# One queue position for the products of v, a larger allowance for table lookups, and earlier weight sums and row turns in a fused attention and feed-forward kernel

## The chip, the cores and the metric

The kernel runs on one core of a Trainium2 chip, as one launch. The metric is the device time of that launch in microseconds: the median of three runs of the kernel before is 1821.81 us (1821.67 to 1823.17). Besides these runs there is one execution with the hardware profiler, from which all lines below come.

The core has a matrix engine (TensorE, PE in the profile, with PEld for its weight loads), a vector engine (VectorE, DVE), an activation engine (ScalarE, ACT), a general engine (GpSimd, POOL) and a queue that issues most transfers (SyncE, SP). Each works through its own instructions in the written order and waits on semaphores of the others.

## The reference

All data are f32. `x` is 16 x 256 x 512, `ctx` the same shape, the mask 16 x 1 x 512 of ones (the kernel still applies it).

```python
x = x + xattn(layernorm(x), ctx, mask, mask, Wq, bq, Wk, bk, Wv, bv)   # 16 heads of 16 channels
x = x + ffn(layernorm(x), lut, gate_idx, up_idx, down_idx)

# xattn: q, k, v = W @ input + b;  dot = q.k / 4 per head, masked
#        out = softmax(dot, over s) * mask @ v
# ffn:   w = lut[idx]  (a table of 16 values; 1376 x 512 indices each for gate and up, 512 x 1376 for down)
#        h = silu(x @ gate.T) * (x @ up.T);  out = h @ down.T
```

So the kernel has to look up 2.1 million weights in a table of 16 values, run 256 attention heads of 512 x 512 scores, and run a feed-forward layer with an inner width of 1376 over 4096 rows.

## The kernel before, in words

**Attention.** A unit (`u`, 64 of them) is four heads of one of the 16 batches; it has four steps, one for each 128 rows (256 steps, `s` from 0 to 255). In each step `scores(sa, sb)` (L469) issues two things side by side on TensorE, which holds four 32-row tiles: the scores `pa` of step `sa = s + 7` (L487), from which VectorE takes row maxima `nm` (L503, two reductions a step), and the turned scores `pb` of step `sb = s` (L495), which ScalarE exponentiates into `pt` (L507, four a step). The maximum enters `pb` as an extra row of `qp`. `turn_max(u)` (L509 to L515) turns a unit's maxima with a small product `pmx` (L512), VectorE copies it out as `mx` (L514), and a transfer issued by GpSimd (L515) writes it into `qp`, three steps before it is needed.

Between the scores of two steps stands a lump of other TensorE work: `apply_v` (L529, twice a unit), projections of q and k (L413, pq and pk), and in step `4u - 3` the pair `turn_max(u)` and `project_v` (L413, pv). The lists `lumps[s]` and `after[s]` are filled by hand and run in the order in which they were filled. `project_v` ends in a ScalarE copy `vt` (L453) and a GpSimd addition (L454). All these products take turns in four PSUM banks (`ps_b`); `pa` has two buffers of its own (`ps_a`). Every eighth step GpSimd multiplies and adds finished rows (`finish_rows`, L584 and L585).

**Lookups.** `look_up` makes weights from indices with VectorE alone: four bit masks (L146, L150), eight leaves (L157) and seven joins (L161, COPY_PREDICATED). Up to step `turns - 3` = 229 the pieces are wide, 128 x 688 (`lookups_early`); what is left of them at step 229 is issued there at once, `load_rest` then issues the load of the first piece of 128 x 344 (`idx_r`, L705), and `lookups_late` goes on. How many lookup operations a step gets is decided by `credit` (L767): each step adds 1930 ns plus `lasting[s]` (the lumps) and takes off `taken[s]` (other VectorE work) and 2590 ns for the reductions.

**Feed-forward.** The rows are eight blocks of 512 rows. Gate and up are done for pairs of blocks `p` = 0 to 3 and column groups `o` of 128 (the last has 96): the column group 0 of the first four blocks by plain products (`gate_up`, L914), everything else by `unit(p, o)`, which has seven products of half the depth in place of eight (L934), in the order 1, 6, 2, 7, 5, 4, 3, with VectorE additions (L938) between them. This needs sums of weights (`combine_w`, L830: `sw` and a changed `wu`) and sums of turned rows for each pair (`combine_x`, L839 to L842: `xe` and a changed `xT`). Product 6 needs the second of the four sums of both, product 7 the third sum of weights.

`fill(ns)` hands out VectorE work from the generator `between()`: sums of weights by column ranges (128 to 384, 384 to 688, then 688 to 1024 after five lookups, 1024 to 1376 after five more, and 0 to 128 last), and lookups between and after them. It adds `ns` to `room[0]`, which is cut to 3000, and issues work until the room is used up. Where a column group needs sums that are not issued yet, a loop in front of the unit (`while o not in ready`) issues all that is missing at once; that can happen for `o` 5 and 8. The units run in the order (0,1), (1,1), (0,2), ... (1,7), then pair 0 with `o` 8 to 10, pair 1 with 8 to 10, then pairs 2 and 3 with all of theirs; the fourteenth counted from zero is (0,8), the nineteenth is (1,10), the twentieth (2,0). Each unit runs three hooks: after product 6, after product 7 and after product 4. `turn_blocks` puts the norm and turning of the rows of a later pair into such hooks: nine steps, the last of which turns the last rows and then issues the four operations of `combine_x`.

After that comes the down product (L1121, L1140, L1145), which the change leaves as it is.

Of the kernel before, what the change touches and what calls it, by code (L numbers as in the profile page):

```python
# [19 lines left out]
def kernel(  # L20
# [46 lines left out]
    NU = 2 * NK  # L67
# [117 lines left out]
    def load_x2(k):  # L185
        x2s[k] = rpool.tile([P, T], F32, tag="x2", name=f"x2t_{k}", bufs=4)
        nc.sync.dma_start(x2s[k], x2_d[k])
        return x2s[k]
# [30 lines left out]
    with ExitStack() as att:  # L219
# [53 lines left out]
        def load_b(b):  # L273
            xn = p2.tile([P, NCC, T], F32, tag="xn", name=f"xn_{b}")
            nc.sync.dma_start(xn, x[b].rearrange("(o p) t -> p o t", p=P))
            cx = p2.tile([P, NCC, T], F32, tag="ctx", name=f"ctx_{b}")
            nc.sync.dma_start(cx, src[b].rearrange("(o p) t -> p o t", p=P))
            mb = p2.tile([P, T], F32, tag="mb", name=f"mb_{b}")
            nc.sync.dma_start(mb, mask[b, 0].partition_broadcast(P))
            inp[b] = (cx, xn, mb)  # L280

        def norm1(b, eng):
            xn = inp[b][1]
            for o in range(NCC):
                i = b * NCC + o
                eng.tensor_scalar(
                    xn[:, o, :], xn[:, o, :], rstd1[:, i : i + 1], nmr1[:, i : i + 1],
                    ALU.mult, ALU.add,
                )
# [30 lines left out]
        for i, w in enumerate((bq, bk)):  # L320
            for e in range(2):
                at = 64 * i + 32 * e
# [6 lines left out]
        for i, w in enumerate((bq, bk)):  # L329
            at = n + NCC * i  # L330
# [114 lines left out]
        def project_v(k, i):  # L445

            b, half = divmod(k, 2)
            cx = inp[b][0]
            c = 2 * half + i
            ps = ps_b.tile([P, 512], F32, tag="b", name=f"pv_{b}_{c}")  # L450
            in_columns(ps[:, :C], lambda o, at: cx[:, o, at], c * P, lambda o: wv[:, o, :])
            vt = p2.tile([P, C], F32, tag="vt", name=f"vt_{b}_{c}")
            nc.scalar.copy(vt, ps[:, :C])  # L453
            nc.gpsimd.tensor_tensor(  # L454
                vas[b % 2][:, c, :, 0:D], vt.rearrange("p (h d) -> p h d", d=D),
                bvb.rearrange("p (h d) -> p h d", d=D), ALU.add,
            )

        def mask_v(k, i):
            b, half = divmod(k, 2)  # L460
            c = 2 * half + i
            va = vas[b % 2][:, c, :, 0:D]
            m = cols[:, b * NCH + c : b * NCH + c + 1]
            nc.scalar.activation(va, va, AF.Copy, scale=m)
# [44 lines left out]
        def turn_max(u):  # L509
            ps = ps_b.tile([P, 512], F32, tag="b", name=f"pmx_{u}")  # L510
            nms.pop(u)
            nc.tensor.matmul(ps[:32, :P], nm32[u % 2], ident, start=True, stop=True)  # L512
            mx = p2.tile([4 * NCH, P], F32, tag="mx", name=f"mx_{u}")
            nc.vector.tensor_copy(mx, ps[: 4 * NCH, :P])  # L514
            nc.gpsimd.dma_start(qps[u % 4][17 : P : 32, :].rearrange("j (c t) -> j c t", t=P), mx)  # L515
# [73 lines left out]
        lumps, after = defaultdict(list), defaultdict(list)  # L589
# [32 lines left out]
            after[t + 18].append(lambda k=k: spread_sums(k))  # L622
            after[t + 20].append(lambda k=k: finish_rows(k))

        for u in range(NU):
            lumps[4 * u - 3].append(lambda u=u: turn_max(u))
        lumps[-3].append(lambda: project_v(0, 0))
        lumps[-2] += [lambda: project_v(0, 1), lambda: project_v(1, 0)]
        lumps[-1].append(lambda: project_v(1, 1))
# [1 line left out]
        for k in range(2, NK):  # L631
            for i in range(2):
                lumps[8 * k - 15 + 4 * i].append(lambda k=k, i=i: project_v(k, i))
                after[8 * k - 13 + 4 * i].append(lambda k=k, i=i: mask_v(k, i))
        for b in range(2, B):
            after[16 * b - 31].append(lambda b=b: load_b(b))
            after[16 * b - 23].append(lambda b=b: norm1(b, nc.gpsimd))
# [8 lines left out]
        taken = defaultdict(float)  # L646
# [55 lines left out]
        def load_rest():  # L702
            w, idx, h, k = rest[0]
            its[0] = lp.tile([P, WIDE], I32, tag="idx", name=f"idx_r{len(rest)}", bufs=2)
            nc.sync.dma_start(its[0][:, :PIECE], idx[h * P : (h + 1) * P, k * PIECE : (k + 1) * PIECE])  # L705
# [19 lines left out]
        credit = 0.0  # L725
# [16 lines left out]
        lasting = defaultdict(float)  # L742
# [9 lines left out]
        for s in range(min(min(after), min(lumps)), NSTEP + 2):  # L752
            sa = s + AHEAD if 0 <= s + AHEAD < NSTEP else None
            sb = s if 0 <= s < NSTEP else None
            if sa is not None or sb is not None:
                scores(sa, sb)
            for fn in lumps.pop(s, ()):
                fn()
            for fn in after.pop(s, ()):
                fn()  # L760
            if s >= 0:
                if s == turns - 3:
                    for _, op in early:
                        op()
                    load_rest()
                queue = early if s < turns - 3 else late
                credit += 1930 + lasting[s] - taken[s] - (2590 if sa is not None else -500)  # L767
                credit = min(credit, 1500.0)
                if s == NSTEP - 6:
                    closing.append(s)  # L770
                while credit > 0:
                    ns, op = next(queue, (0, None))
                    if op is None:
                        break
                    op()
                    credit -= ns
# [18 lines left out]
    with ExitStack() as ffn:  # L795
# [14 lines left out]
        def rows_of(o):  # L810
            return min(P, INTER - o * P)
# [22 lines left out]
        def combine_x(p):  # L834

            x1, x2 = xTs[2 * p], xTs[2 * p + 1]
            b11, b21, b12, b22 = x1[:, 0:2], x1[:, 2:4], x2[:, 0:2], x2[:, 2:4]
            xe = xes[p] = xep.tile([P, 3, 2, 4 * P], F32, tag="xe", name=f"xe_{p}")
            yield v.tensor_tensor(xe[:, 0], b22, b12, ALU.subtract)  # L839
            yield v.tensor_tensor(b12, b12, b11, ALU.subtract)  # L840
            yield v.tensor_tensor(xe[:, 1], b22, b12, ALU.subtract)
            yield v.tensor_tensor(xe[:, 2], b21, xe[:, 1], ALU.subtract)  # L842
# [53 lines left out]
        def fill(ns):  # L896

            room[0] = min(room[0] + ns, 3000.0)
            while room[0] > 0:
                took, op = next(todo, (0, None))  # L900
                if op is None:
                    break
                op()
                room[0] -= took


        def gate_up(n, o):

            rows = rows_of(o)
            at = slice(o * P, o * P + rows)  # L910
            ps = ps_a.tile([P, 2, 512], F32, tag="a", name=f"pgu_{n}_{o}")
            for i, w in enumerate((wg, wu)):
                for h in range(NH):
                    nc.tensor.matmul(  # L914
                        ps[:rows, i, :], w[:, h, at], xTs[n][:, h, :],
                        start=(h == 0), stop=(h == NH - 1),
                    )
            sg = rpool.tile([P, 4 * P], F32, tag="us0", name=f"sg_{n}_{o}", bufs=5)
            nc.scalar.activation(sg[:rows], ps[:rows, 0, :], AF.Silu)
            ht = f1.tile([P, 4 * P], F32, tag="ht", name=f"ht_{n}_{o}")  # L920
            v.tensor_tensor(ht[:rows], sg[:rows], ps[:rows, 1, :], ALU.mult)
            store_h(n, o, ht, rows)
# [49 lines left out]
        order = [(p, o) for o in range(1, 8) for p in range(2)]  # L972
        order += [(p, o) for p in range(2) for o in range(8, NO)]
        order += [(p, o) for p in range(2, 4) for o in range(NO)]
        hooks = defaultdict(list)

        def turn_blocks(n, at):

            k = 4 * n

            def step(i):
                if i:
                    turn2(k + i - 1)
                if i < 8:
                    norm2(k + i)
                    room[0] -= 550
                if i + 3 < 8:
                    load_x2(k + i + 3)
                if i == 8:
                    for _ in combine_x(n // 2):  # L990
                        room[0] -= 1230

            for i in range(3):
                hooks[at - 1, 2].append(lambda i=i: load_x2(k + i))
            for i in range(9):
                hooks[at + i // 3, i % 3].append(lambda i=i: step(i))

        turn_blocks(4, order.index((1, 8)))
        turn_blocks(6, order.index((2, 5)))
        for i in range(8):  # L1000
            for n, at in ((4, 8), (6, 15)):
                hooks[at + i, 0].append(lambda k=4 * n + i: load_x2(k))
# [5 lines left out]
        k = 4 * FIRST  # L1008
# [3 lines left out]
            fn()  # L1012
        load_x2(k + 2)
        load_x2(k + 3)
        gate_up(0, 0)
        gate_up(1, 0)
        turn2(k)
# [7 lines left out]
        gate_up(2, 0)  # L1025
        turn2(k + 2)
        turn2(k + 3)
        fill(6000)
        gate_up(3, 0)
        for _ in combine_x(1):  # L1030
            pass
        fill(3000)

        def run(fns):
            for fn in fns:
# [201 lines left out]
```

## Time and profile before

| what | value |
|---|---|
| median of three runs | 1821.81 us |
| the profiled execution, its own time | 1821.44 us |
| its span, first to last instruction | 1819.7 us |
| TensorE busy | 1796.0 us (99%) |
| VectorE busy | 1459.0 us (80%) |
| ScalarE / GpSimd busy | 799.5 / 491.5 us |
| attention, first feed-forward product | to about 993 us |
| units of gate and up | about 1025 to 1540 us |
| granted TensorE clock | 0.999 over the span |

The span is 1.7 us shorter than the execution's own time, and 2.1 us shorter than the median. The parts of the page that matter here are the busy times, the chain of work that ended last, and the waits; the timeline shows single instructions. A line of the timeline has the start in us, the duration in us, the engine, the line of the kernel, the operation, what it writes and reads, how many follow each other, and in brackets the idle time of the engine before it and what ended it. TensorE instructions overlap, so a group's duration is the stretch that it covers.

### The profile page before, as it was taken

The page shows a single profiled execution, that of the slowest core. Times are in us where ns is not written, and L with a number is a line of the kernel's source. Part 1 is how long each engine was busy: PE and PEld are TensorE (multiplying, and loading weights), DVE is VectorE, ACT ScalarE, POOL GpSimd, SP SyncE. Part 2 cuts the span into 40 slices and gives each one's busy share as a digit, 9 for nine tenths or more (in the row PEclk, how much of TensorE's full clock was granted, in tenths as well). Part 3 has the DMA queues.
Part 4 walks back from the last instruction along what each step waited for, and adds up shares of the span by engine and source line. Part 5 has one row for each costly group of instructions (what it writes and reads, how often), then busy time and mean ns, then how long its engine had stood idle before and what let it go on. Part 6 is the DMA issues. An engine that isn't in the chain of part 4 may idle for free.

```text
span 1819.7 us, 28550 instructions
## 1 busy us (share of the span) xinstructions
PE 1796.0 (99%) x10914; PEld 812.4 (45%) x10914; DVE 1459.0 (80%) x2030; ACT 799.5 (44%) x1523; POOL 491.5 (27%) x467
## 2 busy tenths in 40 slices
PE   8999999999999999999999999999999999999999
PEld 4333333333333333333234444444444444588887
DVE  6898988889898889898886799998888995353352
ACT  1777777777777777777676111112121111000000
POOL 4333343434333433433322122222222222000000
PEclk9999999999999999999999999999999999999999
DMA  6445534333433344444242211223231311533541
GB/s 187 129 143 149 149 115 129 121 114 96 127 114 125 92 128 137 148 121 141 87 120 75 69 58 55 74 81 106 68 104 42 116 51 44 182 132 126 176 132 58
DMA packets 118825, 201.07 MB, mean 111 GB/s; under 512 B 21781, under 2 KB 23961, under 8 KB 118689
## 3 DMA queue, kind: packets, MB, share of 16 engines
q1 hardware_dynamic: 114416, 196.21, 34.1%
q0 software_dynamic: 3168, 1.86, 0.5%
q8 instruction: 86, 1.41, 0.3%
q10 hardware_dynamic: 1104, 1.19, 0.2%
q14 instruction: 51, 0.41, 0.1%
HBM read 135.83 MB, written 58.10 MB: 107 GB/s over the span
## 4 chain that ended last, share of the span: by engine, by line
PE 92%; DVE 4%; DMA 1%; issue 0%; ACT 0%; SPq 0%; POOL 0%; ACTq 0%; DVEq 0%; POOLq 0%
PE p L934 27%; PE pa L487 15%; PE pv L529 12%; PE pb L495 11%; PE q L1140 11%; PE pv L413 3%; PE pq L413 3%; PE pk L413 3%; PE po L1121 2%; DVE nm L503 2%; PE q L1145 1%; PE pgu L914 1%; PE pmx L512 1%; PE pt L215 1%; DMA x2t<-x 1%; DVE chosen L161 0%
## 5 line engine op out<-in xcount | busy, mean ns | idle before, releaser
L503 DVE TENSOR_REDUCE nm<-pa 128x2 f32<-128x1024 f32 x512 | 603.3, 1220 | 103.8 <-PE pb L495 97.5
L507 ACT ACTIVATE pt<-pb 128x512 f32<-128x512 f32 x1024 | 530.0, 603 | 108.8 <-PE pb L495 107.7
L487 PE MATMUL pa<-kp,qp 32*128 32x512 f32 x2048 | 515.0, 616 | 9.5 <-DVE nm L503 6.9
L495 PE MATMUL pb<-qp,kp 32*128 32x512 f32 x2048 | 514.9, 617 | 0.0
L487 PEld LDWEIGHTS pa<-kp,qp 32*128 32x128 f32 x2048 | 179.5, 184 | 208.7 <-DVE nm L503 163.1
L529 PE MATMUL pv<-pt,va 128*32 128x512 f32 x2048 | 246.2, 598 | 0.0
L495 PEld LDWEIGHTS pb<-qp,kp 32*128 32x128 f32 x2048 | 203.4, 183 | 83.5 <-issue 52.4
L934 PE MATMUL p<-xe,wu 128*128 128x512 f32 (+1 forms) x336 | 158.1, 593 | 1.0 <-DVE w L938 1.0
L934 PE MATMUL p<-xT,sw 128*128 128x512 f32 (+1 forms) x336 | 157.9, 592 | 0.0
L934 PE MATMUL p<-xT,wg 128*128 128x512 f32 (+1 forms) x336 | 157.9, 592 | 0.0
L961 POOL TENSOR_TENSOR ha<-ha,sg 128x512 f32<-128x512 f32 (+1 forms) x42 | 60.4, 1438 | 344.3 <-DVE ha L938 326.0
L966 ACT ACTIVATE w<-w 128x512 f32<-128x512 f32 (+1 forms) x42 | 26.5, 630 | 241.4 <-DVE w L938 241.4
L529 PEld LDWEIGHTS pv<-pt,va 128*32 128x32 f32 x2048 | 53.4, 109 | 173.1 <-ACT pt L507 97.1
L515 POOL DMA_DIRECT2D qp<-mx x64 | 37.8, 591 | 313.1 <-DVE mx L514 290.4
L1156 ACT COPY q<-q 128x256 f32<-128x256 f32 x14 | 5.2, 372 | 254.4 <-PE q L1140 254.4
L534 ACT COPY us<-pv 128x512 f32<-128x512 f32 x128 | 74.9, 585 | 91.7 <-PE pv L529 91.0
L934 PEld LDWEIGHTS p<-xe,wu 128*128 128x128 f32 (+1 forms) x336 | 62.8, 187 | 83.0 <-issue 71.3
L934 PEld LDWEIGHTS p<-xT,wg 128*128 128x128 f32 (+1 forms) x336 | 62.7, 187 | 79.2 <-issue 75.4
L934 PEld LDWEIGHTS p<-xT,sw 128*128 128x128 f32 (+1 forms) x336 | 62.1, 187 | 75.4 <-issue 73.9
L948 ACT ACTIVATE sg<-sg 128x512 f32<-128x512 f32 (+1 forms) x42 | 26.5, 631 | 152.4 <-DVE sg L938 152.4
L541 POOL TENSOR_TENSOR us<-us,us 128x512 f32<-128x512 f32 x64 | 82.3, 1286 | 16.5 <-ACT us L534 16.5
L429 POOL TENSOR_TENSOR natk<-natk,mb 128x512 f32<-128x512 f32 x31 | 40.0, 1289 | 157.7 <-ACT natk L426 152.0
(205 smaller groups left out, 2375.1 us busy)
## 6 DMA issues: line engine op xcount, KB each, us to landing
x2t<-x SPq DMA_DIRECT2D x96, 256.0 KB
h<-h SPq DMA_DIRECT2D x7, 2560.0 KB
kp<-kd SPq DMA_DIRECT2D x62, 256.0 KB
qp<-qd SPq DMA_DIRECT2D x62, 256.0 KB
h<-ha SPq DMA_DIRECT2D x38, 256.0 KB
h<-hb SPq DMA_DIRECT2D x38, 256.0 KB
rb<-rd SPq DMA_DIRECT2D x32, 256.0 KB
xr<-in_x_dram SPq DMA_DIRECT2D x32, 256.0 KB
```

The source lines that it names most:

```text
L413: nc.tensor.matmul(ps[32 * j : 32 * j + 32], weights(o, slice(first + 32 * j, first + 32 * j + 32)), moving(o), start=(o == 0), stop=(o == ...
L429: nc.gpsimd.tensor_tensor(t, t, mb, ALU.mult)
L487: nc.tensor.matmul(pa[:, jj, :], qps[ua % 4][at, ca * P : (ca + 1) * P], kps[ua % 4][at, :], start=True, stop=True,)
L495: nc.tensor.matmul(pb, kps[ub % 4][at, cb * P : (cb + 1) * P], qps[ub % 4][at, :], start=True, stop=True,)
L503: nc.vector.tensor_reduce(nms[ua][:, 2 * half : 2 * half + 2, ca], pa, AX.X, ALU.max, negate=True)
L507: nc.scalar.activation(pts[sb][:, j, :], pb, AF.Exp)
L529: nc.tensor.matmul(ps[32 * j : 32 * j + 32, :], va[:, at : at + 32], pt[:, j, :], start=(i == 0), stop=(i == 1),)
L534: nc.scalar.copy(us[u, half], ps)
L541: nc.gpsimd.tensor_tensor(a, a, b, ALU.add)
L934: nc.tensor.matmul(ps, a[:, h, at], b[:, h, :], start=h == 0, stop=h == 1)
L961: nc.gpsimd.tensor_tensor(ha, ha, sg, ALU.mult)
L1140: nc.tensor.matmul(ps, a[:, o, first_t], b[:, o, :], start=o == 0, stop=o == HO - 1 and not more,)
```

## The change

Six edits, all in the order or amount of work; no arithmetic changes.

1. The loop that puts `turn_max(u)` into `lumps[4u - 3]` stands after the loops that put `project_v` there. In those lumps the product for v comes first, then the turning of the maxima.
2. The reductions are taken off `credit` at 2565 in place of 2590, so that each step hands out 25 ns more of lookups.
3. `turn_blocks` counts in hooks in place of units, and the steps for blocks 4 and 5 (pair 2) come one hook sooner; those of pair 3 stay.
4. `fill(6500)` in front of the first `gate_up`.
5. `fill(2500)` in place of `fill(6000)` in front of the fourth `gate_up`.
6. `combine_x(1)` is no longer issued whole in front of the units with a `fill(3000)` behind it; its four operations go into the hooks of the first unit, each with `fill(-1230)`.

```diff
-        for u in range(NU):
-            lumps[4 * u - 3].append(lambda u=u: turn_max(u))
+
         lumps[-3].append(lambda: project_v(0, 0))
         lumps[-2] += [lambda: project_v(0, 1), lambda: project_v(1, 0)]
         lumps[-1].append(lambda: project_v(1, 1))
...
                 lumps[8 * k - 15 + 4 * i].append(lambda k=k, i=i: project_v(k, i))
                 after[8 * k - 13 + 4 * i].append(lambda k=k, i=i: mask_v(k, i))
+        for u in range(NU):
+            lumps[4 * u - 3].append(lambda u=u: turn_max(u))
...
-                credit += 1930 + lasting[s] - taken[s] - (2590 if sa is not None else -500)
+                credit += 1930 + lasting[s] - taken[s] - (2565 if sa is not None else -500)
...
             for i in range(3):
-                hooks[at - 1, 2].append(lambda i=i: load_x2(k + i))
+                hooks[divmod(at - 1, 3)].append(lambda i=i: load_x2(k + i))
             for i in range(9):
-                hooks[at + i // 3, i % 3].append(lambda i=i: step(i))
-
-        turn_blocks(4, order.index((1, 8)))
-        turn_blocks(6, order.index((2, 5)))
+                hooks[divmod(at + i, 3)].append(lambda i=i: step(i))
+
+        turn_blocks(4, 3 * order.index((1, 8)) - 1)
+        turn_blocks(6, 3 * order.index((2, 5)))
...
         load_x2(k + 3)
+        fill(6500)
         gate_up(0, 0)
...
-        fill(6000)
+        fill(2500)
         gate_up(3, 0)
-        for _ in combine_x(1):
-            pass
-        fill(3000)
+        second = combine_x(1)
+        for i in range(4):
+            hooks[0, min(i, 2)].append(lambda: (next(second, None), fill(-1230)))
```

## The prediction

> **What bounds the kernel now.** I read the page first, then the timeline where TensorE pauses, then windows of one microsecond for the clock and the transfers.
>
> ```profile
> PE 1796.0 (99%) x10914; PEld 812.4 (45%) x10914; DVE 1459.0 (80%) x2030; ACT 799.5 (44%) x1523; POOL 491.5 (27%) x467
> PE 92%; DVE 4%; DMA 1%; issue 0%; ACT 0%; SPq 0%; POOL 0%; ACTq 0%; DVEq 0%; POOLq 0%
> ```
>
> TensorE is the bound; what can be won is its pauses, mostly waits for VectorE (the 4% of the chain). One regular lump:
>
> ```profile
> 210.27 2.06 ACT L507 ACTIVATE pt<-pb 128x512 f32<-128x512 f32 x4 [0.42 <-PE pb L495]
> ...
> 210.99 0.14 PEld L512 LDWEIGHTS pmx<-ident,nm 128*32 128x32 f32 x2 [0.76 <-ACT pt L507]
> ...
> 211.40 0.59 PEld L413 LDWEIGHTS pv<-wv,ctx 128*32 128x32 f32 x16 [0.27 <-ACT pt L507]
> ...
> 212.40 0.18 PEld L487 LDWEIGHTS pa<-kp,qp 32*128 32x128 f32 x1 [0.41 <-issue]
> ```
>
> The turned maxima take 0.41 us of TensorE, the product for v 1.00. The latter waits for the second exponential to free its bank. The next scores start 0.07 us after the fourth exponential (210.27 + 2.06 = 212.33). The lookups left at step 229:
>
> ```profile
> 892.37 2.34 DVE L503 TENSOR_REDUCE nm<-pa 128x2 f32<-128x1024 f32 x2
> 894.62 0.27 DVE L514 COPY mx<-pmx 16x128 f32<-16x128 f32 x1
> 894.82 1.17 DVE L157 TENSOR_SCALAR chosen<-chosen,lut_x,lut_b 128x688 int32<-128x688 int32 x2
> 896.02 3.83 DVE L161 COPY_PREDICATED chosen<-chosen,chosen 128x688 int32<-128x688 int32 x2
> 899.88 0.92 DVE L161 COPY_PREDICATED wg<-idx,chosen 128x688 int32<-128x688 int32 x1
> 900.70 2.34 DVE L503 TENSOR_REDUCE nm<-pa 128x2 f32<-128x1024 f32 x2
> ...
> 903.45 0.33 DVE L146 TENSOR_SCALAR late_xn<-idx_r 128x344 int32<-128x344 int32 x1
> ```
>
> Five lookup operations stand in front of two reductions that free the buffers of the scores. TensorE is idle from 898.0 to 901.97, and afterwards its clock falls (column before the last two):
>
> ```profile
> 897.00:898.00 1.00, 0.94 (x12) 0.03 (x4) 1.00 (x1) 0.19 (x1) 1.00 (x1) 1.00 0.34 121
> 898.00:899.00 1.00, 0.00 (x0) 0.00 (x0) 0.97 (x2) 0.58 (x1) 0.08 (x1) 1.00 0.00 0
> ...
> 903.00:904.00 1.00, 1.00 (x8) 0.49 (x8) 0.97 (x5) 0.83 (x2) 0.00 (x0) 0.59 0.00 0
> 904.00:905.00 1.00, 1.00 (x8) 0.00 (x0) 0.91 (x1) 0.25 (x1) 0.00 (x0) 0.50 0.05 8
> 905.00:906.00 1.00, 1.00 (x12) 0.26 (x12) 0.76 (x1) 0.81 (x2) 0.00 (x0) 0.50 0.09 16
> 906.00:907.00 1.00, 1.00 (x12) 0.26 (x8) 0.96 (x4) 0.28 (x1) 0.00 (x0) 0.70 0.37 92
> ```
>
> The queue's side, and three places in the feed-forward units:
>
> ```profile
> 893.48 0.42 SPq L705 DMA_DIRECT2D idx_r<-in_L_ffn_gate_idx_dram  x1
> 900.83 0.33 SPq L705 DMA_DIRECT2D idx_r<-in_L_ffn_up_idx_dram  x1
> ...
> 1034.44 1.98 PE L934 MATMUL p<-xe,wu 128*128 128x512 f32 x4 [0.70 <-DVE w L938]
> ...
> 1193.29 0.88 DVE L830 TENSOR_TENSOR wu<-wg,wu 128x704 f32<-128x704 f32 x1
> 1194.09 1.96 DVE L830 TENSOR_TENSOR sw<-wg,sw 128x704 f32<-128x704 f32 x1
> ...
> 1268.90 2.11 DVE L839 TENSOR_TENSOR xe<-xT 128x1024 f32<-128x1024 f32 x1 [0.37 <-ACT xT L216]
> ...
> 1273.59 1.98 PE L934 MATMUL p<-xe,sw 128*128 128x512 f32 x4 [1.91 <-DVE xe L841]
> ```
>
> The same sum of weights takes 0.88 us alone and 1.96 while GpSimd multiplies.
>
> **The change part by part.** The order of instructions on each engine, built from the changed source, tells where work lands. I sum against the profiled execution's 1821.44 us (span 1819.7); the median of the runs is 0.37 higher.
>
> *v before the maxima (60 lumps).* The product for v then takes the bank that the first exponential has already freed, so its wait of 0.27 goes, and the turn (two passes, 0.13 apart) ends the lump about 0.17 earlier. But the second turned score needs the bank of the fourth exponential, done at 212.33, where it now starts at 212.42. With the 0.05 that a bank takes to be seen (the second exponential ends at 211.35, the load follows at 211.40), 0.04 us a lump is left: 60 x 0.04 = -2.4. Bounds: 60 x 0.27 = -16 if nothing else held the scores, and on the other side the maxima. Their copy is ready as before, since it stands behind reductions to 212.68; but on GpSimd their transfer now stands behind the addition for v (0.73 us) and leaves some 0.45 later. The page's median from issue to landing is 3.5 us, and two steps of 3.78 less 0.74 leave 6.8, so a lump pays only where the transfer is slow: I take +0.2, at most 0.45 at each of the 15 steps behind a batch's loads, +7.
>
> *25 ns a step.* By step 229 that is 5.7 us of lookups, the whole remainder: in the changed order the wide pieces end at step 225. They sit in earlier steps, where VectorE has 1.42 us free in a step of 3.78 (reductions 2.36). Only a lump of 1.41 behind an overfull step pays, and GpSimd's `finish_rows` makes every eighth step overfull: a leaf and a join there end 0.97 late and cost 0.58 (685, 774, 863 us: 0.13 to 0.15 and 0.45), two leaves 0.21 (567 us), two joins 1.04 (596 us), a mask and a leaf about 0.2, two masks about 0.05. Before: four leaf-join cases, counting 507 us at 0.55, one of two leaves, one of two joins, 3.6 us. After, by the order: four leaf-join, three two-leaf, two mask-leaf, seven two-mask: 3.7. Sum +0.1, between -1 and +2.
>
> *The remainder gone.* Before, 893 to 908 us costs 0.60 (scores 2.38 against 1.93, v 1.15 against 1.00), 4.10 (5.95 against 1.85), 1.19 (scores 3.12) and 0.72 (pk 2.58): 6.6, of which the clock (0.41 + 0.50 + 0.50 + 0.30 missing in four windows) 1.7. What is late next is the load of `idx_r`: its first mask follows the maxima at once, at about 894.0, in front of the next reductions. SP issues that load behind stores and row loads, at 893.48, as before; transfers run until 898 and then stop, so it lands at up to 897.9. Two masks of 0.33 and one reduction of 1.2 follow, the scores start at 899.8 in place of 897.26: +2.55. The lower bound is the second load, issued at 900.83 and over by 903.0: landing at 895.7, +0.35. I take 2.55, since the transfers show it. The idle time is then nearer to the 1.91 us at 1273.59, behind which the clock stayed at 1.00, than to the 4.0, so no clock loss; with it +1.7. Net -4.05. A late leaf in place of a join (GpSimd beside it, 1.61 us) at 919.7 saves 0.7 of the 1.07 lost there.
>
> *Start of the units.* Five sums of weights go to VectorE at 992, where it idled 9.0 us; the second pair's sums of rows go between the first unit's additions (4 x 1.26 beside 7 x 0.65 in 12 us), the third of them some 0.5 us ahead of its product. The 0.70 at 1034.44 goes: -0.70, at worst 0.
>
> *Rows of the third pair.* The four sums start behind product 7 of the nineteenth unit, at 1265.05 (row copy to 1265.0), without GpSimd beside them, and end at 1270.1. Then come a row statistic (0.87) and two additions that read product 5, done at 1272.2. Product 6 of the next unit needs that bank and could start at 1271.1: 1.15 lost in place of 1.91. Sum -0.75, between -1.91 and 0.
>
> *Sums of weights, the part that goes wrong.* The first unit's sums are now charged to the room, 4 x 1230, so lookups and the sums of columns 1024 to 1376 slip back by about a unit. In the changed order none of the latter stands in front of unit 14; the loop in front of unit 14, the first of column group 8, issues all four at once, behind the last addition of unit 13, a leaf and three joins. Before, two of the four stood early in unit 13 and the others behind product 4. Product 6 of unit 14 reads the second sum. With the present times of these units: the addition ends at 1195.8 (held by GpSimd, as at 1183.15), leaf and joins take 0.37 + 3 x 0.46 + 1.3 for GpSimd's second multiplication (a join of 0.55 took 1.64 at 1184.59), two sums 1.7: 1200.4, against a start at 1195.91. That is +4.5; without any GpSimd time it is 1.3 + 0.6 less, +2.65. TensorE idles longer than the 4.0 us of 898, so the clock falls as it did there, +1.7.
>
> Sum: -2.2 + 0.1 - 4.05 - 0.7 - 0.7 - 0.75 + 4.5 + 1.7 = -2.1 us: 1819.4.
>
> [...]
>
> **The rivals.**
>
> A. The scores after a lump do not hang on the fourth exponential, and the lump's whole 0.17 shows: 60 x 0.17 = 10.2 in place of 2.4, so 1811.6. For it: TensorE's own sequence gives 212.40 too. Against it: the exponentials end 0.07 before.
>
> B. The stop in front of unit 14 is short: no GpSimd in the way (2.65), or no fall of the clock: 1815.9 to 1817.7. For it: nothing but alignment; against it: the 1.96 and 0.50 rows.
>
> C. Slower: the later transfer of the maxima makes TensorE wait in lumps with busy queues. 0.45 at 15 lumps is +6.8, less the 0.2 counted 1826.0; it decides from 6 us of such waits on, 0.4 at each of the 15. Against it: the 3.5 us of the page against 6.8, and ends of slow transfers that are set by what is queued ahead of them, which does not move.
>
> D. The clock falls behind the wait for `idx_r` too: 1821.1, the same as before.
>
> **How the numbers follow.** About 0.2% (3.6 us) is what a measurement tells from no change: below 1818.2 is faster, above 1825.4 slower. The sum as it stands has 0.38 (0.33 within, 0.05 below by its small terms), A 0.10, B 0.26, C 0.13, D 0.13. Faster 0.05 + 0.10 + 0.26 = 0.41, same 0.33 + 0.13 = 0.46, slower 0.13. The range from 1811.5 (A) to 1823.5 leaves C out, and part of A.
>
> **What would show it.** Right: in lumps L413 pv comes first with no wait, and the scores start 3.30 after those before, in place of 3.34; no L161 x2 in front of the reductions near 900, but an idle VectorE ended by `idx_r`; TensorE idle some 4.5 us in front of an L934 of column group 8, ended by L830 (L831 in the changed file), with PEclk 0.50 behind it; 1.1 us in front of the first unit of pair 2. Wrong: scores at 3.2 after the last, new waits of pb for a transfer, or a stop in front of unit 14 under 2 us.

## The result, and the profile after

The changed kernel takes 1825.74 us (median of 20 runs, 1822.71 to 1830.62), the kernel before, beside it, 1822.38. The ratio is 1.0014 (95% interval 1.0008 to 1.0021): slower by 0.14%, where 1819.4 was forecast; it lies above the range, which ended at 1823.5. The profiled execution took 1823.87 us with a span of 1822.1, 2.4 more than before.

The page of the changed kernel, its busy times and the shares of the chain that ended last:

```profile
PE 1796.0 (99%) x10914; PEld 840.8 (46%) x10914; DVE 1461.8 (80%) x2030; ACT 793.6 (44%) x1523; POOL 505.6 (28%) x467
PE 89%; DVE 4%; DMA 2%; issue 1%; POOL 0%; SPq 0%; ACT 0%; POOLq 0%; ACTq 0%; DVEq 0%
```

TensorE has the same work and the pauses are again waits for VectorE, but at other places. GpSimd is 14 us longer busy with the same instructions, a first sign that its operations now stand at other places beside VectorE's: 9.5 of the 14 are in the moved addition (L454), which takes 1.19 to 1.59 us in 13 of its 64 places and about 0.74 elsewhere, where before it took at most 0.75.

I set the start of each attention step and of each feed-forward unit of one execution beside that of the other, and noted where the difference changes:

| part | forecast | measured |
|---|---|---|
| start-up, to the first steps | 0 | -0.4 |
| 60 lumps, v in front of the maxima | -2.4 | -2.5 |
| what the moved transfer and the moved addition cost | +0.2 | +2.1 |
| overfull steps, 61 to 227 | +0.1 | +0.4 |
| the remainder at 890 to 925 us | -4.75 | -1.9 |
| the lump at 930 us, which gives nothing back | 0 | -0.2 |
| start of the units | -0.7 | -0.96 |
| unit 14 | +6.2 | +6.53 |
| third pair | -0.75 | -1.08 |
| down product | 0 | +0.4 |
| sum, and the difference of the spans | -2.1 | +2.4 |

The +2.1 are three stalls of 0.84, 0.75 and 0.81 us (at 68, 238 and 262 us), less some 0.3 in small gains. The rows of the start-up and the down product need not be the change's doing: two executions of one and the same kernel (all3 and rep_again below) differ by 1.4 and 0.6 us there.

The lump that answers to the one at 210 us, from the timeline:

```profile
209.90 2.07 ACT L507 ACTIVATE pt<-pb 128x512 f32<-128x512 f32 x4 [0.42 <-PE pb L495]
...
210.62 0.59 PEld L413 LDWEIGHTS pv<-wv,ctx 128*32 128x32 f32 x16 [0.76 <-ACT pt L507]
...
211.30 0.33 PEld L512 LDWEIGHTS pmx<-ident,nm 128*32 128x32 f32 x2
...
211.82 0.18 PEld L487 LDWEIGHTS pa<-kp,qp 32*128 32x128 f32 x1 [0.20 <-issue]
...
212.01 0.29 PEld L495 LDWEIGHTS pb<-qp,kp 32*128 32x128 f32 x2
...
212.31 0.73 POOL L454 TENSOR_TENSOR va<-vt,bvb 128x256 f32<-128x256 f32 x1 [2.62 <-ACT vt L453]
...
212.97 0.59 POOL L515 DMA_DIRECT2D qp<-mx  x1
```

The wait of 0.27 is gone. The scores start 0.15 before the fourth exponential ends (209.90 + 2.07 = 211.97), and then take 2.10 instead of 1.93, because their second half needs that exponential's bank (its weights are loaded at 212.01): 0.21 won in one step, 0.17 given back in the next, 0.042 in all. On GpSimd the addition now stands in front of the transfer.

The place of the former remainder, timeline and then windows of one microsecond (the number before the last two is the TensorE clock):

```profile
893.22 0.43 SPq L706 DMA_DIRECT2D idx_r<-in_L_ffn_gate_idx_dram  x1
...
898.24 0.34 DVE L146 TENSOR_SCALAR late_xn<-idx_r 128x344 int32<-128x344 int32 x1 [4.43 <-DMA idx_r<-in_L_ffn_gate_idx_dram]
...
898.74 2.35 DVE L503 TENSOR_REDUCE nm<-pa 128x2 f32<-128x1024 f32 x2
...
900.02 0.69 PE L487 MATMUL pa<-kp,qp 32*128 32x512 f32 x1 [2.98 <-DVE nm L503]
```

```profile
900.00:901.00 1.00, 0.98 (x8) 0.31 (x8) 1.00 (x1) 0.00 (x0) 0.00 (x0) 1.00 0.02 8
901.00:902.00 1.00, 1.00 (x8) 0.52 (x8) 0.93 (x5) 0.78 (x2) 0.00 (x0) 0.52 0.00 0
...
904.00:905.00 1.00, 1.00 (x12) 0.32 (x8) 1.00 (x3) 0.38 (x1) 0.00 (x0) 0.78 0.61 53
```

VectorE idles 4.43 us for a load that needed 5.0 us from its issue to its first use, the reductions stand behind two masks of it, TensorE pauses for 2.98 us, and the clock is at one half from 901.03 to 904.45 all the same (such a stretch is called a half clock below).

The stop in front of unit 14, and the first unit of the third pair:

```profile
1193.05 1.30 POOL L968 TENSOR_TENSOR hb<-hb,w 128x512 f32<-128x512 f32 x1 [1.54 <-ACT w L967]
1193.28 1.46 DVE L161 COPY_PREDICATED tb_l<-b_l,tc_l 128x344 int32<-128x344 int32 x1
...
1195.35 0.89 DVE L831 TENSOR_TENSOR sw<-wu 128x704 f32<-128x704 f32 x1
1196.28 0.89 DVE L831 TENSOR_TENSOR sw<-sw,wg 128x704 f32<-128x704 f32 x1
...
1197.22 3.05 PE L935 MATMUL p<-xe,sw 128*128 128x512 f32 x4 [4.56 <-DVE sw L831]
...
1275.63 1.98 PE L935 MATMUL p<-xe,sw 128*128 128x512 f32 x4 [0.83 <-DVE hb L939]
```

```profile
1197.00:1198.00 1.00, 0.78 (x2) 0.49 (x3) 1.00 (x3) 0.00 (x0) 0.00 (x0) 1.00 0.64 242
1198.00:1199.00 1.00, 1.00 (x2) 0.34 (x1) 1.00 (x2) 0.00 (x0) 0.00 (x0) 0.50 0.00 0
```

A join beside GpSimd's multiplication takes 1.46 (the one behind it, with nothing beside it, 0.54), two sums 1.8, product 6 stops for 4.56 us, and the half clock follows. The product itself, a row of four passes, takes 3.05 us, where the one at 1275.63 takes 1.98.

And a place that the prediction did not look at, in the lump step at 64 us:

```profile
64.17 0.72 POOL L454 TENSOR_TENSOR va<-vt,bvb 128x256 f32<-128x256 f32 x1 [5.21 <-ACT vt L453]
...
64.28 0.63 DVE L119 SCALAR_TENSOR_TENSOR nwt<-rstd,nwt 128x2 f32<-128x2 f32 x1
...
65.33 1.70 DVE L131 SCALAR_TENSOR_TENSOR nmr<-mv,rstd 128x2 f32<-128x2 f32 x1
65.70 1.30 POOL L541 TENSOR_TENSOR us<-us,us 128x512 f32<-128x512 f32 x1
...
66.95 2.34 DVE L503 TENSOR_REDUCE nm<-pa 128x2 f32<-128x1024 f32 x2
...
68.22 0.18 PEld L487 LDWEIGHTS pa<-kp,qp 32*128 32x128 f32 x1 [1.41 <-DVE nm L503]
```

L119 to L131 are small VectorE operations, 128 x 2, that refine the reciprocal roots for the norm of coming rows. L131 starts 0.37 us in front of GpSimd's addition of 1.30 and ends with it (67.03 and 67.00): it takes 1.70 us. The reductions behind it are late, and TensorE with them. Before, there was no pause here (timeline of before):

```profile
65.30 0.16 DVE L131 SCALAR_TENSOR_TENSOR nmr<-mv,rstd 128x2 f32<-128x2 f32 x1
...
65.73 0.73 POOL L454 TENSOR_TENSOR va<-vt,bvb 128x256 f32<-128x256 f32 x1
```

That may have been a narrow escape: L131 started 0.43 us in front of the addition there, and at 109 and 258 us, where it started 0.39 and 0.36 in front, it took 2.39 and 2.61 us in the kernel before too. At 262 us the same operations, 128 x 20 there, cost the step 1.0 before and 0.98 more with the change. The 1.0 us at 68 and the 0.98 at 262 include the 0.17 that every lump gives back.

### The profile page after: what moved, and what is told of

Read it like the earlier page. It is cut to its first block, busy times and chain, and to the rows that moved or that the text cites. A ratio compares the mean times of both kernels' runs of the same rounds, so it can differ in the third digit from the quotient of the medians.

```text
span 1822.1 us, 28542 instructions
## 1 busy us (share of the span) xinstructions
PE 1796.0 (99%) x10914; PEld 840.8 (46%) x10914; DVE 1461.8 (80%) x2030; ACT 793.6 (44%) x1523; POOL 505.6 (28%) x467
## 3 DMA queue, kind: packets, MB, share of 16 engines
q10 hardware_dynamic: 1104, 1.19, 0.2%
## 4 chain that ended last, share of the span: by engine, by line
PE 89%; DVE 4%; DMA 2%; issue 1%; POOL 0%; SPq 0%; ACT 0%; POOLq 0%; ACTq 0%; DVEq 0%
PE p L935 27%; PE pa L487 15%; PE pv L529 12%; PE pb L495 11%; PE q L1142 10%; PE pk L413 3%; PE pq L413 3%; PE pv L413 3%; PE po L1123 2%; DVE nm L503 2%; DMA x2t<-x 1%; PE q L1147 1%; PE pgu L915 1%; PE pt L215 1%; PE pmx L512 1%
## 5 line engine op out<-in xcount | busy, mean ns | idle before, releaser
L487 PE MATMUL pa<-kp,qp 32*128 32x512 f32 x2048 | 523.3, 617 | 9.5 <-DVE nm L503 7.7
L487 PEld LDWEIGHTS pa<-kp,qp 32*128 32x128 f32 x2048 | 191.3, 184 | 199.7 <-DVE nm L503 161.4
L495 PEld LDWEIGHTS pb<-qp,kp 32*128 32x128 f32 x2048 | 220.3, 183 | 67.6 <-issue 41.8
L454 POOL TENSOR_TENSOR va<-vt,bvb 128x256 f32<-128x256 f32 x64 | 56.7, 886 | 247.8 <-ACT vt L453 237.9
```

Source lines behind the costliest of these rows:

```text
L454: nc.gpsimd.tensor_tensor(vas[b % 2][:, c, :, 0:D], vt.rearrange("p (h d) -> p h d", d=D), bvb.rearrange("p (h d) -> p h d", d=D), ALU.add,)
L487: nc.tensor.matmul(pa[:, jj, :], qps[ua % 4][at, ca * P : (ca + 1) * P], kps[ua % 4][at, :], start=True, stop=True,)
L495: nc.tensor.matmul(pb, kps[ub % 4][at, cb * P : (cb + 1) * P], qps[ub % 4][at, :], start=True, stop=True,)
```

## Experiments

Three theories. **The stop:** the weight sums that are forced in front of unit 14 are the loss. **The swap:** the new order on GpSimd is. **The remainder:** the gain that was to pay for all this stayed in the wait for `idx_r`. The changes to the profiled time of one execution are compared place by place, since its start-up alone differs by up to 3 us between executions. In the table, "before" is the kernel before on the same chip.

| kernel | median, us | before | ratio (95%) | profiled, us |
|---|---|---|---|---|
| ffn_only | 1827.13 | 1822.14 | 1.0029 (1.0018 to 1.0040) | 1826.28 |
| att_only | 1820.94 | 1822.14 | 0.9997 (0.9988 to 1.0006) | 1820.66 |
| swap_only | 1822.25 | 1822.14 | 1.0007 (0.9997 to 1.0018) | 1823.72 |
| credit_only | 1821.59 | 1822.14 | 0.9994 (0.9984 to 1.0003) | 1819.77 |
| no_charge | 1819.29 | 1823.62 | 0.9979 (0.9970 to 0.9988) | 1821.89 |
| idx_soon | 1819.92 | 1823.62 | 0.9981 (0.9972 to 0.9989) | 1820.14 |
| pool_order | 1823.64 | 1823.62 | 0.9994 (0.9985 to 1.0003) | 1823.91 |
| all3 | 1811.39 | 1823.62 | 0.9933 (0.9920 to 0.9945) | 1811.39 |
| rep_again | 1812.94 | 1822.74 | 0.9947 (0.9934 to 0.9959) | 1812.94 |
| rep_no_swap | 1815.49 | 1822.74 | 0.9959 (0.9947 to 0.9972) | 1813.89 |
| rep_2590 | 1819.76 | 1822.74 | 0.9978 (0.9967 to 0.9989) | 1819.93 |
| rep_old_start | 1813.84 | 1822.74 | 0.9952 (0.9940 to 0.9964) | 1813.81 |

### The parts alone

**ffn_only:** the kernel before with edits 3 to 6. Its diff is the second half of the one shown, from `load_x2` in the hooks on.

> Edits 3 to 6 alone on the kernel before (rows of the third pair one hook sooner, the sums in front of and in the first unit); attention as before. Theory 1 (the stop in front of unit 14 is what turned the change into a loss): the feed-forward part carries its own loss of -0.96 (start of the units) + 6.5 (unit 14: an idle TensorE of 4.6 us ended by a sum of weights, then a clock of 0.50) - 1.1 (third pair) + 0.4 (down product) = +4.9, so 1826.3 against the profiled execution of before at 1821.44, ratio 1.0027, all of it found again at the same places. Theory 2 (the stop is made longer by what comes from the attention edits): the stop in front of unit 14 is shorter or the clock stays up, at most +3.

Measured: +4.84 in the profiled execution, ratio 1.0029. Unit 0 gives -0.96, unit 14 +6.53, the third pair -1.08, each as in the changed kernel to 0.01; the rest is +0.5 in the start-up, +0.5 in attention, where the half clock behind the pause at 898 us lasts 6.83 us in this execution, and -0.6 in the down product. The first theory holds at every place that it names; that its total is met to 0.1 is luck. The stop does not depend on anything in attention.

**att_only, swap_only, credit_only:** the kernel before with edits 1 and 2, with 1, and with 2. The loop of `turn_max` moves behind those of `project_v`; the second pair of lines is the credit.

```diff
-        for u in range(NU):
-            lumps[4 * u - 3].append(lambda u=u: turn_max(u))
...
+        for u in range(NU):
+            lumps[4 * u - 3].append(lambda u=u: turn_max(u))
...
-                credit += 1930 + lasting[s] - taken[s] - (2590 if sa is not None else -500)
+                credit += 1930 + lasting[s] - taken[s] - (2565 if sa is not None else -500)
```

> Edits 1 and 2 alone on the kernel before (v in front of the turned maxima, 25 ns a step more for the lookups); feed-forward as before. Theory 1: the gain of attention that the changed kernel showed, -2.45 us at the end of attention, stands alone: 1819.0, ratio 0.9987. Theory 2 (what attention gains is lost again in the feed-forward part, whatever stands there): no difference, 1821.4.

> Edit 1 alone on the kernel before. Lumps give 60 x 0.04 = -2.4. Theory 1 (the swap also costs: the addition for v on GpSimd in front of the transfer of the maxima moves GpSimd's work against the small operations of the reciprocal roots at 64, 109 and 258 us and delays a transfer at 231 us): those cost +1.7 and +0.75 here, so the sum is 0, 1821.5, with a stall of 1.4 behind a reduction at about 68 us and one of 0.9 at about 237 us. Rival (those stalls come from the lookups that the other edit hands out sooner): none of these stalls, 1819.0, ratio 0.9987.

> Edit 2 alone on the kernel before: 25 ns a step more for the lookups. No wide operations are left at 900 us; a wait for idx_r takes their place, with the half clock behind it: -1.5 to -1.9 there. Theory 1: the overfull steps cost +0.8 and nothing else moves, sum -0.9, 1820.5. Rival (the lookups handed out sooner cause the stalls at 64 to 68, 231 to 238 and 258 us too): +2.4 more, 1822.9.

att_only: ratio 0.9997, with an interval that takes in no difference and ends just above the first theory's 0.9987. From the first steps to the end of attention it gains 1.2 (the changed kernel, with the same order of instructions there, 2.0), and from there to the end of the units nothing changes (-0.168 both times): the second theory's mechanism falls, and the first one's size is too large by about one us.

swap_only: the stalls of 1.0 at 68 us and 0.97 at 262 us are there, the one at 237 us is 0.27 instead of 0.75, and the ratio takes in 1. credit_only: no difference at 68, 238 or 262 us (0.00, -0.17, +0.01); the overfull steps sum to +0.3 and the place at 890 us to -1.7; its profiled time of 1819.77 stands near the first theory's 1820.5. So the stalls belong to the swap and not to the lookups, and the swap alone wins nothing that can be measured.

One line of swap_only is about the clock. The pause of 1.91 us in front of the first unit of the third pair, behind which the clock stayed at 1.00 in the kernel before, is followed by half the clock here (timeline, then windows):

```profile
1274.22 3.43 PE L935 MATMUL p<-xe,sw 128*128 128x512 f32 x4 [1.91 <-DVE xe L842]
```

```profile
1274.00:1275.00 1.00, 0.78 (x2) 0.41 (x3) 0.97 (x2) 0.00 (x0) 0.00 (x0) 0.81 0.00 0
1275.00:1276.00 1.00, 1.00 (x3) 0.48 (x2) 1.00 (x2) 0.00 (x0) 0.00 (x0) 0.50 0.00 0
```

It cost 1.70 there. The same idle time had two outcomes, so its length alone does not decide (more on this in the last section).

### The changed kernel with one cause taken away

**no_charge**

```diff
-            hooks[0, min(i, 2)].append(lambda: (next(second, None), fill(-1230)))
+            hooks[0, min(i, 2)].append(lambda: (next(second, None), fill(0)))
```

> The changed kernel, but the four sums of rows in the first unit are not charged to the room (fill(0) in place of fill(-1230)), so that the weight sums of columns 1024 to 1376 fall into units 12 and 13 again, one by one. Theory 1 (the stop in front of unit 14 is all of the loss): the idle 4.6 us and the 1.7 us of half clock behind it go, -6.5 against the changed kernel's profiled execution of 1823.87, so 1817.4; a lookup or two more beside the first unit's sums may give 0.7 back. Ratio to the kernel before 0.998. Theory 2 (the work that fills those units is late in any case and stops TensorE elsewhere): a new pause of 2 us or more at units 0 to 5, 1821 or more.

Measured: ratio 0.9979, where the changed kernel had 1.0014. Place by place, unit 14 is 6.53 faster and no other unit changes. The profiled time fell by 2.0 only, as this execution has 5.2 us more by the end of attention: 2.8 in its start-up and 1.6 at 267 us, each with a half clock, and 0.8 in small amounts. The first three weight sums now stand alone between the additions (0.88 us each), and the products of unit 14 follow each other without a wait (timeline of no_charge):

```profile
1193.99 0.88 DVE L831 TENSOR_TENSOR sw<-sw,wg 128x704 f32<-128x704 f32 x1
...
1196.02 1.88 PE L935 MATMUL p<-xT,wg 128*128 128x512 f32 x4
1197.74 1.88 PE L935 MATMUL p<-xe,sw 128*128 128x512 f32 x4
```

The second sum ends at 1194.9, 2.9 us ahead of the product that reads it. Theory 1 holds.

**idx_soon:** the first late piece is loaded like every other, while the piece in front of it is worked on.

```diff
                 if i + 1 < len(pieces):
                     load_wide(i + 1)
+                else:
+                    load_rest()
...
                     for _, op in early:
                         op()
-                    load_rest()
```

> The changed kernel, with the load of the first late piece (idx_r) issued when the last wide piece is begun, some 90 us sooner. Theory 1 (the wait for idx_r keeps most of what the removed wide lookups should have given): the idle stretch of 2.98 at 897 and the half clock behind it (1.8) go, -4.7, so 1819.2 against 1823.87, and the masks of idx_r end before the reductions want VectorE. Theory 2 (VectorE is overfull there whatever it waits for): the pause stays above 2 us, at most -1.

Measured: ratio 0.9981; attention ends 4.1 us sooner; 4.8 are won between 898 and 921 us, and 0.7 are lost in small amounts in front of them. (Unit 14 happens to cost 0.9 more: its half clock lasts 6.83 us in this execution.) The idle stretch shrinks from 2.98 to 0.41 and no half clock follows. The masks did not quite end in time:

```profile
895.05 1.93 DVE L150 TENSOR_SCALAR late_xn<-idx_r 128x344 int32<-128x344 int32 x1
895.48 1.29 POOL L541 TENSOR_TENSOR us<-us,us 128x512 f32<-128x512 f32 x1
...
898.16 0.69 PE L487 MATMUL pa<-kp,qp 32*128 32x512 f32 x1 [0.41 <-DVE nm L503]
```

A mask of 0.33 takes 1.93 and ends at 896.98, again about when GpSimd's addition is over (896.77). Theory 1 holds, less that 0.4.

**pool_order:** GpSimd's addition for v leaves `project_v` and stands behind the transfer again.

```diff
             nc.scalar.copy(vt, ps[:, :C])
+            vts[k, i] = vt
+
+        vts = {}
+
+        def add_v(k, i):
+            b, half = divmod(k, 2)
+            c = 2 * half + i
             nc.gpsimd.tensor_tensor(
-                vas[b % 2][:, c, :, 0:D], vt.rearrange("p (h d) -> p h d", d=D),
+                vas[b % 2][:, c, :, 0:D], vts.pop((k, i)).rearrange("p (h d) -> p h d", d=D),
...
         for u in range(NU):
             lumps[4 * u - 3].append(lambda u=u: turn_max(u))
+        for k in range(2, NK):
+            for i in range(2):
+                lumps[8 * k - 15 + 4 * i].append(lambda k=k, i=i: add_v(k, i))
```

> The changed kernel, with TensorE's order as changed (v, then the turned maxima), but on GpSimd the transfer of the maxima in front of the addition for v again, as before the change. Theory 1 (the later transfer and the moved additions cause the stalls at 67, 238 and 262 us): those of 1.0, 0.75 and 1.0 go, the lumps keep their 0.04, so -2.7: 1821.2 against 1823.87, and no idle stretch of 1.7 at 261 us. Theory 2 (they come from the times at which the small operations of VectorE fall, which TensorE's order alone sets): the three stalls stay, 1823.9.

Measured: the three stalls are 0.84, 0.92 and 0.77 shorter, and 0.27 comes back at 113 us and 0.6 in overfull steps; after the first steps attention is 1.7 faster than in the changed kernel. Theory 1 holds for the stalls, at 1.7 of its 2.7 in all. The profiled time is the same only because its start-up is 2.6 longer, with a half clock at 18 us. The ratio is 0.9994 against 1.0014. The step at 64 us, now at 67 (timeline of pool_order):

```profile
66.83 0.14 DVE L119 SCALAR_TENSOR_TENSOR nwt<-rstd,nwt 128x2 f32<-128x2 f32 x1
...
67.19 0.60 POOL L522 DMA_DIRECT2D qp<-mx  x1 [5.69 <-DVE nwt L120]
...
67.39 0.16 DVE L131 SCALAR_TENSOR_TENSOR nmr<-mv,rstd 128x2 f32<-128x2 f32 x1
...
67.48 2.36 DVE L510 TENSOR_REDUCE nm<-pa 128x2 f32<-128x1024 f32 x2
...
67.82 0.73 POOL L461 TENSOR_TENSOR va<-vt,bvb 128x256 f32<-128x256 f32 x1
```

(With this edit the lines from 461 on stand seven later: L510 is the reduction, L519 the turned maxima, L522 the transfer, L494 the scores, L461 the addition for v.) L131 runs beside GpSimd's issue of the transfer, 0.43 in front of the addition, and takes 0.16; L119 has nothing beside it and takes 0.14. The additions follow when VectorE is in its reductions. At 262 us the meeting itself stays, as in the kernel before: L131 starts 0.35 in front of the addition and takes 2.60. What goes there is what the change had added.

At 238 us the cause is the transfer. In the changed kernel the moved addition stands in front of it and meets a join (timeline of the changed kernel):

```profile
226.95 1.57 POOL L454 TENSOR_TENSOR va<-vt,bvb 128x256 f32<-128x256 f32 x1 [5.22 <-ACT vt L453]
227.06 0.91 DVE L161 COPY_PREDICATED wg<-chosen,chosen 128x688 int32<-128x688 int32 x1
...
228.47 0.58 POOL L515 DMA_DIRECT2D qp<-mx  x1
```

The addition takes 1.57 in place of 0.73, and the transfer is issued 1.99 us behind the start of the scores at 226.48; before, it was 0.74 behind them. It takes, in the view of the tile `qp`,

```profile
DMA to landing us min/median/max: 6.5/6.5/6.5
```

so it lands at 234.97, 0.76 behind the start of the step that needs it (234.21), and that step's scores come 0.93 late instead of 0.17. In pool_order the issue is at 229.40 for a step that starts at 236.18, and nothing waits. In all nine profiled kernels that keep the transfer in front of the addition on GpSimd, none of the 64 additions takes over 0.75; in the five others 13 to 15 of them take 1.19 to 1.60.

**all3:** these three edits together.

> The three of this call together on the changed kernel. If they are independent: -6.5 - 4.7 - 2.7 = -13.9 against 1823.87, so 1810.0, ratio to the kernel before 0.994. If the repairs of attention only shift work into the next overfull step, 1813 or more.

Measured: 1811.39 us, ratio 0.9933. Against the changed kernel the profiled time is 12.5 less, 13.7 from the first steps on; the independent sum was 13.9. They even help each other: with GpSimd's order repaired the first two masks of `idx_r`, at 893.5 us, take 0.32 each, and the pause of 0.41 that idx_soon kept is gone. The profiled execution has no half clock behind its start-up:

```profile
PE 1791.0 (99%) x10914; PEld 839.2 (46%) x10914; DVE 1455.7 (80%) x2030; ACT 793.9 (44%) x1523; POOL 496.6 (27%) x467
PE 92%; DVE 3%; DMA 1%; issue 0%; ACT 0%; SPq 0%; POOL 0%; ACTq 0%; POOLq 0%; DVEq 0%
```

This is the version that beats both kernels.

### What each edit is worth once its obstacle is gone

The kernel with the repairs, again, and with one edit of the change undone each time: the maxima in front of v on TensorE, 2590 in the credit, and `fill(6000)`, the whole `combine_x(1)` and `fill(3000)` as before.

> The kernel with the three repairs once more, beside the next three on one chip: 1811.3 as its profiled execution was, ratio to the kernel before 0.993. A ratio above 0.996 would mean that the first figure was luck with the clock.

> The kernel with the three repairs, with the turned maxima in front of v on TensorE again; GpSimd's order is the same in both. Theory 1 (with GpSimd's order repaired the swap is worth its 60 x 0.04): +2.4 against the kernel with the repairs, about 1813.7, ratio 0.9945, and the scores of the step behind a lump start 3.34 after those before, in place of 3.13, and take 1.93 in place of 2.10. Theory 2 (the lumps' 0.04 is paid back by the steps that become overfull, since the copy of the maxima falls later against the lookups: four steps at 0.13): +1.9 or less; down to 0 the swap would not be worth anything.

> The kernel with the three repairs, with 2590 in the credit again. Theory 1 (the lookups handed out sooner are worth what the prediction read, 6.6, less 0.8 in the overfull steps, once idx_r is there): an idle stretch of 4 us near 890 and a half clock of 3.41 us behind it come back, +5.8: about 1817.1, ratio 0.9965. Theory 2 (the early load alone was the gain): +1 at most.

> The kernel with the three repairs, with the start of the units as before the change (edits 4 to 6 undone; the third pair's hooks stay). Theory 1 (the start is worth the 0.96 that unit 0 showed, and nothing else moves): +0.96, about 1812.3. Theory 2 (it is worth nothing once the first unit's sums are not charged): 0. The ratio can't tell these apart; the start of the second unit can, by 0.9 in one execution.

rep_again: 0.9947 with 1812.94; it stands (its execution has a half clock at 18 us).

rep_no_swap: medians 2.6 apart, but the intervals of the ratios overlap. In the profiled executions attention is longer from the first steps on, by 4.1 than in all3 and by 3.4 than in rep_again, but 1.08 of it is a pause at 915 us that rep_old_start shows too, with the attention of all3; 2.3 to 3 remain. Sixty times 0.04 is 2.4: theory 1, by the place-by-place reading alone. The lump has its wait again, and the scores start 212.11 where the fourth exponential ends at 209.98 + 2.06 = 212.04 (timeline of rep_no_swap):

```profile
210.70 0.14 PEld L519 LDWEIGHTS pmx<-ident,nm 128*32 128x32 f32 x2 [0.76 <-ACT pt L514]
...
211.11 0.59 PEld L413 LDWEIGHTS pv<-wv,ctx 128*32 128x32 f32 x16 [0.27 <-ACT pt L514]
...
212.11 0.18 PEld L494 LDWEIGHTS pa<-kp,qp 32*128 32x128 f32 x1 [0.41 <-issue]
```

rep_2590: 6.8 by the medians; 7.9 in the profiled executions from the first steps on, against all3 and rep_again alike. The idle 4.03 us come back with a half clock of 6.83 us, twice the usual (timeline of rep_2590):

```profile
901.42 1.22 PE L494 MATMUL pa<-kp,qp 32*128 32x512 f32 x1 [4.03 <-DVE nm L510]
```

Theory 1 (5.8), and 1.7 more for the second half of that spell. So the edit of the credit is the largest gain of the change, and credit_only shows that without the early load only about a quarter of it (1.7) is left.

rep_old_start: the second unit starts 0.96 later relative to the first, as theory 1 had it; the ratio can't tell.

## Why the prediction was wrong, point by point

**Right.** The 0.04 a lump, with the fourth exponential as the reason; rival A (the whole 0.17) falls. But the sentence on what would show it was off: the scores do start 3.13 behind those before, and 0.17 is lost inside them. Right too is the stop in front of unit 14, 4.5 + 1.7 forecast, 4.56 idle and +6.53 in all, with its chain: forced sums, a join beside GpSimd, a half clock. (The terms of the 4.5 add up to 1200.55 and not to 1200.4, so that it should read 4.6; the difference decides nothing.) Rival B falls. The start of the units (-0.96 for -0.7) and the third pair (-1.08 for -0.75) came as argued, each 0.3 better. The overfull steps sum to little, +0.4 for +0.1.

**Wrong, "the remainder gone", the step "the idle time is then nearer to the 1.91 us, so no clock loss".** The wait for `idx_r` was found and its end almost hit (898.24 for 897.9). The pause was 2.98 for 2.55, and the clock fell, 1.8. The comparison with the pause at 1273 was the error: its full clock was one draw of two, as swap_only shows. The further 0.7 for a late leaf did not come either, since GpSimd stood beside the leaf (1.40 us at 917.66, beside an addition from 917.54 to 918.87) as it had beside the join (1.61). Together 2.85 of 4.75. This was rival D, held at 0.13; it alone would have given 1821.1.

**Wrong, "v before the maxima", the step "a lump pays only where the transfer is slow: I take +0.2".** It cost 2.1. Rival C's mechanism was real at one place (0.75 at 238 us) and far from its deciding 6 us; that its 1826.0 stands next to the measured median is chance. Even there a term was mis-sized: the transfer left 1.25 us later in its step where the prediction had "some 0.45 later", since it counted the addition in front of it at 0.73 and it took 1.57 beside a join. What was missed is the other side of the same move: on GpSimd a transfer and additions changed places in time against VectorE's small operations, which credit_only and pool_order show to be the cause of the further 1.0 at 68 and 1.0 at 262 us (0.84 and 0.81 without what every lump gives back). The prediction had the price of such a meeting in its own rows (a sum of 0.88 taking 1.96 beside GpSimd) and applied it to the lookups, not to the instructions of the lump steps themselves. Nothing in that part of it lists what VectorE does beside the moved addition.

In the rows of the changed kernel the small operation and the addition beside it end together: L119 at 64.91 and GpSimd's addition at 64.89, L131 at 67.03 and the addition at 67.00. The rows do not show what makes a pair meet like this: by the profile L131 starts 0.37 in front of the addition that it ends with, and one that started 0.43 in front took 0.16.

**The sum.** 4.5 us lie between the forecast and the profiled execution: 2.85 from the remainder, 1.9 from the moved work on GpSimd, 0.3 from the overfull steps, 0.3 from unit 14 and 0.4 from the down product, less 0.3 each for the start of the units and the third pair, 0.4 for the start-up and 0.3 for the lumps, that at 930 us above all. So two steps failed, and together they are more than the whole difference. The medians lie 3.4 apart instead of 2.4; that these medians carry one more half clock than the profiled execution fits the runs' mean clock (0.998 in the profiled one, 0.996 or 0.997 in 14 of the 20) but was not traced.

## What to carry to other kernels

When an instruction stream is reordered on one engine, list for the other engines what now runs beside what at each place, the small operations too (L131 at 65 us took 0.16 us before the change and 1.70 with it); repairing the order on the second engine alone turned a swap without a measurable gain into one worth 2.3 to 3 us by the place-by-place reading (the medians do not separate the two). A lump of work that is taken away uncovers the next wait, and the load behind that wait should be moved with it: the same credit was worth 1.7 us with the late load (credit_only) and about 7 with the early one. What a budget is charged for at one end, here four sums of rows, is missing where the budget was spent before, so follow a charge to the last deadline that it can push work against.

## What the runs showed of the chip that was not expected

A pause of one and the same length was followed by a half clock in one execution and not in another. Between 25 and 1800 us the clock fell once in the kernel before, for 3.41 us (903.18 to 906.60), and twice in the changed kernel, for 3.41 us each (901.03 to 904.45, 1197.99 to 1201.41); in ffn_only, idx_soon and rep_2590 one half clock lasted 6.83 us. All pauses of TensorE over 1 us in this stretch of the profiled executions of the two kernels, with one each of swap_only and rep_2590:

| execution | pause, us | it ends at, us | clock behind it |
|---|---|---|---|
| changed | 1.75 | 262.47 | 1.00 |
| before | 1.91 | 1273.59 | 1.00 |
| swap_only | 1.91 | 1274.22 | 0.50 for 3.41 us |
| changed | 2.98 | 900.02 | 0.50 for 3.41 us |
| before | 4.03 | 901.97 | 0.50 for 3.41 us |
| rep_2590 | 4.03 | 901.42 | 0.50 for 6.83 us |
| changed | 4.56 | 1197.22 | 0.50 for 3.41 us |

What decides at 1.91 us these rows do not show. At half the clock 3.41 us cost 1.70, so the same pause at the same place cost nothing further in one execution and 1.7 us in another, and a single execution can't judge it.
